# Token tiles moved by indirect transfers of GpSimd in a recurrence and mixture-of-experts kernel

## Chip, core and metric

The kernel runs on one core of a Trainium2 chip. The time is that of the device for one execution, in microseconds (us), and the profile is one execution recorded by the hardware profiler. The engines are TensorE (PE; its weight loads are listed apart as PEld), VectorE (DVE), ScalarE (ACT), GpSimd (POOL) and SyncE (SP). They run side by side, each works through its own instructions in order, and they wait for each other through semaphores. SP does no arithmetic here: it is a queue that issues transfers (DMAs) between the device's memory (DRAM) and the on-chip memory (SBUF). Matmul results go to PSUM, a second on-chip memory in banks.

## The reference

Cut to what is computed, for x of 8 batches, 1024 time steps and 256 features:

```python
xn = layernorm(x)
# online learning: W is changed by each time step
v = einsum('bsd,ed->bse', xn, Wkv[256:]) + bkv[256:]
def step(W, (xt, vt)):                 # xt, vt: 8 x 256, one time step of all batches
    y = xt @ W.T
    gW = (2 / (8 * 256)) * ((y - vt).T @ xt)
    return W - eta * gW, y
s = scan(step, W0, (xn, v))
# 16 linear experts, the best six of each token weighted by a router
probs = softmax(xn @ router_w.T + router_b)
gate = top-6 of probs, normalised, zero elsewhere
g = silu(sum over e of (xn @ expert_w[e]) * gate[:, e])
out = x + s * g
```

## The kernel before

The 8192 tokens go in 64 tiles of 128 rows: a tile is 16 time steps of all 8 batches, with the time step as the slower index, so row r of tile i is batch r mod 8 and time step 16 i + r div 8. In DRAM, x and the output are ordered by batch, then time step; each of the 128 rows of a tile is a run of 1 KB there.

`load(i)` fetches a tile of x by one DMA of the SP queue (line 100). Two tiles share one buffer of the pool `xin`, which has 10 buffers; at the start the same pool holds the raw weights of the 16 experts (`raw`, line 119), so a tile of x takes over the buffer of an expert whose weights have been split. "Splitting" is line 142 (ACT: the high part `hi` is a rounded copy) and line 143 (DVE or POOL: `lo` is the rest); of the expert weights POOL does the odd experts and DVE the even ones. `layernorm(i)` makes statistics on DVE (`st`, `mv`, lines 194 and 196), `ve` and `rstd` on POOL (lines 198, 200) and `xn` on DVE (line 202). From tile 4 on xn is transposed by way of DRAM: blocks by DVE (`xr`, line 208), one DMA out (`bounce`, line 213) and four DMAs back (`xT`, line 215), all on the SP queue.

TensorE then computes, for each tile, the products with the router and value weights (`vr`, `gram`), small matrix solutions for groups of tiles (`q_ps`, `uq_ps`, `z_ps`, `y_ps`), the recurrence (`pe`, `wt_ps`) and the experts in eight pairs (`h`: six matmuls of 512 columns a pair, in one of three PSUM banks). The results of an expert are weighted and summed: most by DVE (`mix`, line 558), six of the 16 by ACT, which writes `part` (line 547, three buffers), and POOL, which adds the parts up (`mix`, line 550). `finish(i)`, placed one pair into the next tile, joins the sums on DVE (`m`, line 568), multiplies on POOL (`my`, line 572), DVE makes `o` (line 574), POOL adds x to it (line 575; DVE for the last tile), and one DMA of the SP queue stores o (line 576).

The order of TensorE and of the SP queue is written out by hand, as places (tile, pair of experts); a scheduler orders DVE, ACT and POOL around it. On SP the events of one place follow each other, so a load can stand behind a store that waits for its tile, and a bounce behind both:

```python
        fetch = max(4, spot - 21)
        if i >= BY_PE:
            put(fetch // 8, fetch % 8, load, i)
    ctx.enter_context(tc.manual_schedule(engines={mybir.EngineType.PE, mybir.EngineType.SP}))
```

Of the kernel before, what the change touches and what calls it, by code (L numbers as in the profile page):

```python
"""Layer norm, then an online-learned linear layer (one gradient step of W per time step) gated by
the silu of a top-6-of-16 mixture of linear experts, with a residual.

Tokens go in tiles of 128 rows: 16 time steps of all 8 batches, time-major. Within a tile the
recurrence is solved exactly: with A = c * X X^T restricted to strictly earlier time steps and
c = eta * 2 / (B * D), the errors of all steps are E = T (X W^T - V), T = (I + A)^-1, where W is the
weight before the tile, and W^T is then lowered by c * X^T E. The state W^T accumulates in one PSUM
bank.

U = T^T is built for a few tiles at a time from diagonal blocks of 32 rows, by Horner's rule  # L10
(I - C (I - C (I - C)), C = A^T), which merge into blocks of 64 and then 128 rows:
U_ab = -U_a C_ab U_b.

TensorE and the DMA queue keep the order given below; the other engines are scheduled around them.
All but the first tiles are transposed without TensorE: in blocks of 32 by VectorE, and the blocks
change places on their way through DRAM.

The large products split each float32 operand exactly into two float32r parts, x = hi + lo, and add
up hi*hi + hi*lo + lo*hi in float32; what is left out is below float32's own rounding.
"""  # L20

# [8 lines left out]
F32 = mybir.dt.float32  # L30
F32R = mybir.dt.float32r
AF = mybir.ActivationFunctionType
ALU = mybir.AluOpType
AX = mybir.AxisListType
PSUM = bass.MemoryType.PSUM

P = 128
# [3 lines left out]
EPS = 1e-10  # L41
# [9 lines left out]
def ttt_moe_kernel(  # L51
# [12 lines left out]
    nc = tc.nc  # L64
    B, S, D = x.shape
    NE = router_w.shape[0]
    KD = D // P
    TS = P // B
    NT = S // TS
# [21 lines left out]
    where = []  # L91
# [3 lines left out]
    x_tiles = {}  # L95

    def load(i):
        if i % 2 == 0:
            x_tiles[i // 2] = xin.tile([P, KD, D], F32, tag="in", name=f"x_{i // 2}")
        nc.sync.dma_start(  # L100
            out=x_tiles[i // 2][:, i % 2, :],
            in_=x[:, i * TS : (i + 1) * TS, :].rearrange("b t d -> t b d"),
        )
# [9 lines left out]

# [1 line left out]
    raws = {}  # L115
# [23 lines left out]
    nc.gpsimd.memset(neg_half, -0.5)  # L139
    # transposed weights: W0^T the first state, [Wv^T | router^T] one moving operand  # L140
    def split(hi, lo, src, engine=None):
# [41 lines left out]

# [1 line left out]
    class Prepared:  # L185
        pass

    tiles = {}

    def layernorm(i):  # L190
        q = tiles[i] = Prepared()
        xt = x_tile(i)
        st = small.tile([P, nc.vector.BN_STATS_DIM], F32, tag="st", name=f"st_{i}")
        nc.vector.bn_stats(st, xt)  # L194
        mv = small.tile([P, nc.vector.BN_AGGR_DIM], F32, tag="mv", name=f"mv_{i}")
        nc.vector.bn_aggr(mv, st)  # L196
        ve = small.tile([P, 1], F32, tag="ve", name=f"ve_{i}")
        nc.gpsimd.tensor_scalar_add(ve, mv[:, 1:2], LN_EPS)  # L198
        rstd = small.tile([P, 1], F32, tag="rstd", name=f"rstd_{i}")
        nc.gpsimd.tensor_tensor(rstd, ve, neg_half, ALU.pow)  # L200
        q.xn = work.tile([P, D], F32, tag="xn", name=f"xn_{i}", bufs=3)
        nc.vector.tensor_scalar(q.xn, xt, mv[:, 0:1], rstd, ALU.subtract, ALU.mult)  # L202
        if i < BY_PE:
            return
        q.xT = work.tile([P, KD * P], F32, tag="xT", name=f"xT_{i}", bufs=3)
        # blocks of 32 are transposed in place, and change places by way of DRAM
        xr = work.tile([P, D], F32, tag="xr", name=f"xr_{i}")
        nc.vector.transpose(
            xr.rearrange("p (c k t) -> p k c t", c=NQ, k=KD),
            q.xn.rearrange("p (k c t) -> p k c t", c=NQ, k=KD),  # L210
        )
        bounce = dram.tile([NQ, Q, NQ, KD * Q], F32, tag="bounce", name=f"bounce_{i}")
        nc.sync.dma_start(out=bounce.rearrange("b d c f -> (b d) (c f)"), in_=xr)
        for c in range(NQ):
            nc.sync.dma_start(
                out=q.xT[at(c), :].rearrange("p (b f) -> p b f", b=NQ),
                in_=bounce[:, :, c, :].rearrange("b d f -> d b f"),
            )
# [17 lines left out]
    def accumulate(o, hi, lo, rhs_hi, rhs_lo, first=True, **kw):  # L236
        # the terms with the moving low part come last: it is ready last
        terms = [t for a, b, r in zip(hi, lo, rhs_hi) for t in ((a, r), (b, r))]
# [6 lines left out]
    def project(i, g, j):  # L245
        q = tiles[i]
        # X X^T = H H^T + H L^T + (H L^T)^T
        gram = misc(f"gram_{i}")
# [29 lines left out]

# [1 line left out]
    layernorm(0)  # L280
# [10 lines left out]

    # -c at strictly earlier time steps, in A's place and in A^T's
    ones = const.tile([P, P], F32)
# [12 lines left out]

    # U and the first half of T by blocks: what is never written stays zero
    u_full, t_half = [], []
# [10 lines left out]
    def open_group(n, first, count):  # L319
# [14 lines left out]
        for name, t in vars(stores[m]).items():  # L334
            if name in ("t", "z2"):
                setattr(g, name, t)
            else:
                setattr(g, name, t[:, j : j + count])
        # odd tiles keep the first half of T, and what comes of it, in the upper partitions
        g.halves = []  # L340
# [7 lines left out]
    def gates(g):  # L348
# [7 lines left out]

        # the six largest logits, the first of equal ones, are marked; two absent values fill up to eight
        lg, top, d, ex = g.lg, wide("top", 8), wide("d"), wide("ex")
# [16 lines left out]
        nc.vector.tensor_reduce(s_top, chosen, AX.X, ALU.add)  # L375
        # gates p / (sum p + EPS) with p = ex / s_all, then divided by max(their sum, EPS)
        nc.vector.scalar_tensor_tensor(den, s_all, EPS, s_top, op0=ALU.mult, op1=ALU.add)
# [11 lines left out]
    def step_q(g, name, rhs, out):  # L389
        """I - C rhs for the diagonal blocks."""  # L390
        c = g.count
# [69 lines left out]
    H = P // 2  # L461
# [24 lines left out]

# [1 line left out]
    def errors_1(i):  # L488
# [74 lines left out]
    def finish(i):  # L563
        # x + y silu(m) = x + (y / 2) m (1 + tanh(m / 2))
        q = tiles[i]
# [9 lines left out]
        (nc.vector if i == NT - 1 else nc.gpsimd).tensor_add(o, o, xt)  # L575
        nc.sync.dma_start(
            out=out[:, i * TS : (i + 1) * TS, :].rearrange("b t d -> t b d"), in_=o
        )

# [1 line left out]
    opened = {}  # L581
# [17 lines left out]

    # what comes before each (tile, pair of experts)  # L600
    events = {}
# [3 lines left out]

    # the first tiles have a schedule of their own: (slot, pair) as 8 * slot + pair
    chain = {
# [85 lines left out]
```

## Time and profile before

| what | value |
|---|---|
| time, median of 2 runs | 1006.72 us (1005.61 to 1007.83) |
| the profiled execution, first to last instruction | 1004.7 us |
| transfers of x | 64, 128 KB each, 2.7 us from issue to landing |
| transfers of the output | 64, 128 KB each, 2.3 us |
| transfers of bounce and xT | 60 of 128 KB (2.4 us), 240 of 32 KB (1.8 us) |
| DMA traffic | 38.65 MB, 38 GB/s in the mean; 231 GB/s in the first fortieth of the span |
| first tile's experts begin on TensorE | 13.05 us; second tile's 37.49 us |

The profiled execution is timed by its span, first to last instruction; the 2.0 us between it and the median of the runs hold what lies around the span and the spread of the runs. In a line of a group, "x64 | 27.1, 425 | 49.9 <-DMA x" means 64 instructions, 27.1 us busy, 425 ns the mean of one, and 49.9 us of idle time of the engine just before them, ended mostly by the transfer named. In a timeline a row has the start and the duration in us, the engine, the line, the operation, output<-input, and in brackets the idle time before it and what ended it.

### The profile page before, as it was taken

Reading aid. Unit: us, or ns where it says so; the run is one execution under the profiler, and the core shown is the slowest. Engines: PE = TensorE matmul, PEld = TensorE weight load, DVE = VectorE, ACT = ScalarE, POOL = GpSimd, SP = SyncE. Lnnn points to the kernel's source line nnn. Section 1 sums busy time; section 2 is a strip of 40 time slices with the busy share of each in tenths; the row PEclk is TensorE's granted clock in tenths of the full one; section 3 lists DMA queues with packets and bytes.
Section 4 is the critical chain, followed back from the end, with each engine's and each line's share of the span. In section 5 each row is a group of like instructions: output and inputs, shape, how many; then the busy total and the mean of one; then the engine's idle time right before and its main releaser. Section 6 shows DMA issues by size and latency. Waiting matters only on the chain.

```text
span 1004.7 us, 19617 instructions
## 1 busy us (share of the span) xinstructions
PE 977.6 (97%) x6672; PEld 799.9 (80%) x6672; DVE 770.0 (77%) x2225; ACT 436.5 (43%) x1174; POOL 440.8 (44%) x677
## 2 busy tenths in 40 slices
PE   5899999999999999999999999999999999999997
PEld 4677888878888887888878888887888878888785
DVE  7888797777878777787777878778787777867665
ACT  5454444344443534435344443534435344443432
POOL 6544344444344344444444344344444444344333
PEclk8899999999999999999999999999999999999999
DMA  7021111111111111111111111011111111100000
GB/s 231 17 53 49 39 27 43 37 27 43 39 27 42 28 37 43 38 27 44 38 28 43 38 28 43 24 42 43 36 29 43 38 28 43 35 25 11 12 11 11
DMA packets 67092, 38.65 MB, mean 38 GB/s; under 512 B 38176, under 2 KB 66992, under 8 KB 66992
## 3 DMA queue, kind: packets, MB, share of 16 engines
q1 hardware_dynamic: 66992, 37.41, 13.6%
q8 instruction: 52, 0.85, 0.3%
q14 instruction: 48, 0.39, 0.1%
HBM read 21.13 MB, written 16.25 MB: 37 GB/s over the span
## 4 chain that ended last, share of the span: by engine, by line
PE 77%; DVE 14%; issue 2%; POOL 2%; DMA 2%; ACT 2%; SPq 1%; POOLq 0%; DVEq 0%; ACTq 0%
PE h L241 59%; PE pe L241 6%; PE wt_ps L241 4%; PE vr L241 3%; DVE q L407 3%; DVE mix L558 2%; DMA x<-in_L_attn_x_dram 1%; PE gram L250 1%; DVE marked L366 1%; POOL mix L550 1%; DVE st L194 1%; ACT part L547 1%; DVE o L574 1%; DVE d L362 1%; PE uq_ps L395 1%
## 5 line engine op out<-in xcount | busy, mean ns | idle before, releaser
L241 PE MATMUL h<-we,xT_two 128*128 128x512 f32 x3072 | 789.3, 402 | 4.5 <-DVE mix L558 2.5
L241 PEld LDWEIGHTS h<-we,xT_two 128*128 128x128 f32 x3072 | 554.5, 189 | 120.1 <-issue 2.7
L558 DVE SCALAR_TENSOR_TENSOR mix<-h,gate,mix 128x256 f32<-128x256 f32 x576 | 265.6, 475 | 112.0 <-PE h L241 80.1
L547 ACT ACTIVATE part<-h,gate 128x256 f32<-128x256 f32 x384 | 182.1, 474 | 293.1 <-DVE mix L558 171.4
L550 POOL TENSOR_TENSOR mix<-mix,part 128x256 f32<-128x256 f32 x256 | 188.7, 737 | 131.4 <-ACT part L547 124.0
L572 POOL TENSOR_TENSOR my<-m,hy 128x256 f32<-128x256 f32 x64 | 47.3, 739 | 159.0 <-DVE m L568 159.0
L550 POOL TENSOR_TENSOR mix<-part,part 128x256 f32<-128x256 f32 x64 | 47.9, 749 | 72.3 <-ACT part L547 72.3
L575 POOL TENSOR_TENSOR o<-o,x 128x256 f32<-128x256 f32 x63 | 46.5, 738 | 69.4 <-DVE lg L263 59.2
L194 DVE BATCH_NORM_STATS2 st<-x 128x6 f32<-128x256 f32 x64 | 27.1, 425 | 49.9 <-DMA x<-in_L_attn_x_dram 49.5
L241 PE MATMUL vr<-w_vr,xT_two 128*128 128x272 f32 x384 | 59.2, 290 | 0.0
L202 DVE TENSOR_SCALAR xn<-x,mv,rstd 128x256 f32<-128x256 f32 x64 | 49.0, 765 | 12.2 <-POOL rstd L200 11.9
L143 DVE TENSOR_TENSOR wt_lo<-wt_ps,wt_hi 128x512 fp32r<-128x512 f32 x64 | 42.9, 671 | 19.6 <-ACT wt_hi L142 19.5
L142 ACT CAST xT_two<-xT 128x256 fp32r<-128x256 f32 x60 | 24.4, 407 | 71.9 <-PE h L241 69.9
L198 POOL TENSOR_SCALAR ve<-mv 128x1 f32<-128x1 f32 x64 | 14.5, 228 | 91.2 <-DVE mv L196 56.4
L143 POOL TENSOR_TENSOR xn_lo<-xn,xn_hi 128x256 fp32r<-128x256 f32 x64 | 47.7, 746 | 14.2 <-ACT xn_hi L142 13.9
L142 ACT CAST p_hi<-p 128x256 fp32r<-128x256 f32 x64 | 26.0, 406 | 63.6 <-DVE p L498 63.5
L241 PEld LDWEIGHTS vr<-w_vr,xT_two 128*128 128x128 f32 x384 | 52.4, 191 | 0.0
L510 ACT ACTIVATE step_hi<-pe,neg_c 128x256 fp32r<-128x256 f32 x64 | 30.4, 474 | 50.5 <-PE pe L241 50.2
L241 PEld LDWEIGHTS pe<-wt_hi,xT_two 128*128 128x128 f32 x256 | 39.2, 189 | 5.9
L142 ACT CAST wt_hi<-wt_ps 128x512 fp32r<-128x512 f32 x64 | 37.2, 581 | 10.8 <-PE wt_ps L241 10.3
L241 PE MATMUL pe<-wt_hi,xT_two 128*128 128x256 f32 x256 | 40.7, 281 | 0.0
L143 DVE TENSOR_TENSOR p_lo<-p,p_hi 128x256 fp32r<-128x256 f32 x64 | 39.2, 612 | 0.9 <-ACT p_hi L142 0.4
(115 smaller groups left out, 1186.7 us busy)
## 6 DMA issues: line engine op xcount, KB each, us to landing
x<-in_L_attn_x_dram SPq DMA_DIRECT2D x64, 128.0 KB, 2.7
out_dram<-o SPq DMA_DIRECT2D x64, 128.0 KB, 2.3
bounce<-xr SPq DMA_DIRECT2D x60, 128.0 KB, 2.4
xT<-bounce SPq DMA_DIRECT2D x240, 32.0 KB, 1.8
raw<-in_L_ffn_expert_w_dram SPq DMA_DIRECT2D x16, 256.0 KB, 5.0
w_raw<-in_L_attn_Wkv_dram SPq DMA_DIRECT2D x1, 256.0 KB, 3.1
w_raw<-in_L_attn_W_dram SPq DMA_DIRECT2D x1, 256.0 KB, 5.2
bias<-in_L_attn_bkv_dram SPq DMA_DIRECT2D x1, 128.0 KB, 4.5
```

Source lines behind the costliest of these rows:

```text
L142: nc.scalar.copy(hi, src)
L143: (engine or nc.vector).tensor_sub(lo, src, hi.bitcast(F32))
L194: nc.vector.bn_stats(st, xt)
L202: nc.vector.tensor_scalar(q.xn, xt, mv[:, 0:1], rstd, ALU.subtract, ALU.mult)
L241: nc.tensor.matmul(o, lhsT=a, rhs=b, start=first and m == 0, stop=(m == len(terms) - 1), **kw)
L407: nc.vector.tensor_add(g.q1[at(b)], g.a[at(b), :, 1, at(b)], ident_q[at(b), :].unsqueeze(1).broadcast_to([Q, c, Q]),)
L510: nc.scalar.mul(q.step_hi, e, neg_c)
L547: nc.scalar.mul(part, he, gate)
L550: nc.gpsimd.tensor_add(new, q.mix[1], part)
L558: nc.vector.scalar_tensor_tensor(new, he, gate, q.mix[j], op0=ALU.mult, op1=ALU.add)
L572: nc.gpsimd.tensor_mul(my, m, q.hy)
L575: (nc.vector if i == NT - 1 else nc.gpsimd).tensor_add(o, o, xt)
```

## The change

All 64 loads of x and all 64 stores of the output leave the SP queue and become indirect transfers that POOL issues: the 128 rows of a tile are addressed by a column of row numbers in SBUF, in x and in the output seen as 8192 rows of 1 KB. The table of row numbers (`rows`, 128 x 64, one column a tile) is made at the start by two `iota` of POOL and five integer operations of DVE: (r mod 8) * 1024 + 16 i + r div 8. The places of loads and stores in the written order stay in the code, but since only TensorE and SP keep that order, the scheduler now places them among POOL's other work. Comments are dropped as well, which moves line numbers (lines of the changed kernel are 14 to 16 higher).

```diff
+I32 = mybir.dt.int32
...
     def load(i):
         if i % 2 == 0:
             x_tiles[i // 2] = xin.tile([P, KD, D], F32, tag="in", name=f"x_{i // 2}")
-        nc.sync.dma_start(
-            out=x_tiles[i // 2][:, i % 2, :],
-            in_=x[:, i * TS : (i + 1) * TS, :].rearrange("b t d -> t b d"),
+        nc.gpsimd.indirect_dma_start(
+            out=x_tiles[i // 2][:, i % 2, :], out_offset=None,
+            in_=x.rearrange("b s d -> (b s) d"),
+            in_offset=bass.IndirectOffsetOnAxis(ap=rows[:, i : i + 1], axis=0),
         )
...
+    part = const.tile([P, NT], I32)
+    nc.gpsimd.iota(part, pattern=[[0, NT]], base=0, channel_multiplier=1)
+    rows = const.tile([P, NT], I32)
+    nc.vector.tensor_single_scalar(rows, part, B - 1, op=ALU.bitwise_and)
+    nc.vector.tensor_single_scalar(rows, rows, 10, op=ALU.logical_shift_left)
+    nc.vector.tensor_single_scalar(part, part, 3, op=ALU.logical_shift_right)
+    steps = const.tile([P, NT], I32)
+    nc.gpsimd.iota(steps, pattern=[[TS, NT]], base=0, channel_multiplier=0)
+    nc.vector.tensor_tensor(part, part, steps, op=ALU.bitwise_or)
+    nc.vector.tensor_tensor(rows, rows, part, op=ALU.bitwise_or)
...
         (nc.vector if i == NT - 1 else nc.gpsimd).tensor_add(o, o, xt)
-        nc.sync.dma_start(
-            out=out[:, i * TS : (i + 1) * TS, :].rearrange("b t d -> t b d"), in_=o
-        )
+        nc.gpsimd.indirect_dma_start(
+            out=out.rearrange("b s d -> (b s) d"),
+            out_offset=bass.IndirectOffsetOnAxis(ap=rows[:, i : i + 1], axis=0),
+            in_=o, in_offset=None,
+        )
```

## The prediction

> **What bounds the kernel now.** I read the busy times first, then a table of windows, then the waits, then the order in time of the places the change touches. Busy times of the whole profiled execution:
>
> ```profile
> span 1004.7 us, 19617 instructions
> PE 977.6 (97%) x6672; PEld 799.9 (80%) x6672; DVE 770.0 (77%) x2225; ACT 436.5 (43%) x1174; POOL 440.8 (44%) x677
> ```
>
> PE is idle for 27.1 us in all (1004.7 - 977.6): that is the most that any relief of waits could give. The windows show where (busy us of each engine, granted clock, DMA share, GB/s):
>
> ```profile
> 0.00:15.00 15.00, 6.40 (x22) 4.84 (x23) 8.56 (x18) 8.20 (x19) 9.25 (x24) 1.00 0.78 239
> 15.00:30.00 15.00, 11.50 (x67) 8.39 (x66) 14.18 (x41) 8.88 (x25) 9.08 (x10) 0.77 0.56 156
> 30.00:45.00 15.00, 11.73 (x60) 8.79 (x59) 14.16 (x48) 5.91 (x19) 9.57 (x19) 0.91 0.07 20
> ...
> 150.00:210.00 60.00, 59.78 (x415) 49.08 (x415) 46.37 (x136) 25.76 (x69) 26.54 (x41) 1.00 0.14 36
> ```
>
> From 150 us on PE lacks 0.22 us in 60: nothing is left to win there, and POOL has 33.5 of 60 us free. The first 45 us are another kernel: PE lacks 15.4 us of it, DVE is full (14.18 and 14.16 of 15), and POOL is busy for 9 to 10 of 15 with the splits of the expert weights. Two waits concern the moved transfers; first all engines, then the SP queue's own (us in total, times, longest):
>
> ```profile
> DVE st L194 <- DMA x<-in_L_attn_x_dram: 49.5, 41, 3.5
> ```
>
> ```profile
> SPq L576 <- POOL o L575: 616.8, 63, 15.6
> ```
>
> SP stands at the store of a tile for most of the kernel, and the next x load is queued behind it, so DVE waits for x. The change ends both. But PE's 0.22 us in 60 says how little of the 49.5 us reaches PE: over some 900 us at most 3 us. I take 1 us off.
>
> **What is added, and its price.** The built order of the changed kernel has 128 transfers on POOL (64 gathers, 64 scatters). Ahead of the first gather come two index patterns on POOL and five integer operations on DVE, each of 64 columns; DVE is idle until 3.49 us, so they cost only a later first gather, inside the terms below. SP loses 128 issues of about 0.6 us, with its 616.8 us of waiting; nothing on SP was late for PE, so that removal is worth nothing beyond the 1 us.
>
> No POOL transfer is in this trace, so its time on POOL is bounded by rows. From below: SP's own issue of the same 128 KB, 0.60 us (median of the x loads). From above: POOL's longest instruction, a 512-column split at 1.63 us; and far above, 2.7 us, from issue to landing, if POOL were held until the data is there. I take 1.5 us: POOL needs 0.739 us for a 256-column two-input operation that DVE does in 0.417 (m, L568), a factor of 1.77, which makes 1.06 us of SP's 0.60; to it comes a pass over one column of indices, on POOL between 0.228 us (ve) and 0.573 us (rstd), 0.4 in the middle.
>
> The Trainium skill (DMA: Bandwidth & Descriptors, "Latency and other measured facts") gives about 1 us to the first byte of a transfer whose descriptors GpSimd writes, against about 0.6 us for one issued by SP; as an estimate of POOL's time, 1.0 us in place of 1.5 would make the sum below 1021 us in place of 1031.
>
> **The start.** This is where the price falls. POOL before:
>
> ```profile
> 7.71 0.73 POOL L143 TENSOR_TENSOR xn_lo<-xn,xn_hi 128x256 fp32r<-128x256 f32 x1 [2.60 <-ACT xn_hi L142]
> ...
> 22.39 0.22 POOL L198 TENSOR_SCALAR ve<-mv 128x1 f32<-128x1 f32 x1 [3.07 <-DVE total L379]
> ...
> 28.21 1.29 POOL L143 TENSOR_TENSOR we<-raw,we 128x512 fp32r<-128x512 f32 x1 [0.63 <-ACT we L142]
> 29.46 0.73 POOL L550 TENSOR_TENSOR mix<-part,part 128x256 f32<-128x256 f32 x1
> 30.79 0.74 POOL L550 TENSOR_TENSOR mix<-mix,part 128x256 f32<-128x256 f32 x1 [0.59 <-ACT part L547]
> ```
>
> In the built order the loads run far ahead: 12 gathers stand before the last expert split on POOL, 16 before the first sum of two parts (29.46 above), 20 before the second (30.79). Twenty at 1.5 us are 30 us. What can hide them is POOL's waiting in this stretch: 0.70 + 2.60 + 0.38 + 1.19 + 0.67 + 3.07 + 1.46 + 0.63 + 0.59 = 11.3 us if all of it can be used; but these are waits for ACT, DVE and landings that stay in part, and only the first two (3.3 us) lie ahead of the first split. So the second sum is late by 18.7 to 26.7 us, 22.7 in the middle. Also, some gathers reuse the buffer of an expert's raw weights and wait, in POOL's queue, for DVE's split of it; the next splits stand behind them. Before PE feels it there is slack: the second sum ends at 31.53 and frees the buffer for the fifth part, which ACT begins at about 32.2 (0.7 us), and that pair's PSUM bank is wanted next by pair 7, whose matmuls begin at 35.90, 3.1 us after the fifth part ends. 22.7 - 0.7 - 3.1 = 19 us late on PE. Nothing takes it back: from 60 us on PE is full.
>
> The gathers may also hold up DVE. In this stretch two tiny additions show what POOL's splits do to it:
>
> ```profile
> 16.83 2.49 POOL L143 TENSOR_TENSOR we<-raw,we 128x512 fp32r<-128x512 f32 x2
> ...
> 17.20 2.17 DVE L407 TENSOR_TENSOR q<-a,ident_q 32x32 f32<-32x32 f32 x2
> ```
>
> The 32x64 form of these takes 0.215 us elsewhere, so two lost about 1.74 us in 2.49 us of POOL. If a gather did the same, 1.5 us of it would cost up to 1.05 us, 21 us for twenty; nothing at all if it doesn't. I take a quarter, 5 us, since few DVE instructions have two such inputs.
>
> The Trainium skill (SBUF — State Buffer, "Who interferes with whom") says that a DVE instruction with two SBUF inputs is blocked by a GpSimd instruction that reads SBUF, not by one that only writes; the row agrees for the splits, and by the page a transfer that writes descriptors would cost DVE nothing, 1026 us in place of the sum below. The page has a rule against the change as well: GpSimd can't write descriptors while DVE runs a 2-port operation; no row here shows its price.
>
> **The steady state.** On POOL the scatter follows the last addition to o, and in every second tile two gathers follow it, ahead of the first sum of the next tile. Before:
>
> ```profile
> 513.28 0.74 POOL L575 TENSOR_TENSOR o<-o,x 128x256 f32<-128x256 f32 x1 [1.34 <-DVE lg L263]
> 515.28 0.79 POOL L550 TENSOR_TENSOR mix<-part,part 128x256 f32<-128x256 f32 x1 [1.26 <-ACT part L547]
> ```
>
> Three transfers from 514.05 put that sum at 518.55 and its end at 519.3. Its first part's buffer is the one of three that ACT's fourth part takes at 519.59: met by 0.3 us. So at 1.5 us the steady state pays nothing, and the point from which it pays is (519.59 - 0.74 - 514.05) / 3 = 1.6 us.
>
> **The end.** The last scatter is issued by POOL, 1.5 us in place of SP's 0.54, and nothing hides it: +1 us.
>
> **Sum.** 19 + 5 + 0 + 1 - 1 = 24 us on the profiled 1004.7 us. That execution lies 2.0 us below the median of 1006.72, so I add 2.0: 1031 us.
>
> **Rivals.** (1) Cheap transfers, not slower by what can be told: at 0.6 us twenty gathers are 12 us against 11.3 us of waiting. What stays is the order on DVE: tile 0's normalisation now stands behind the split of expert 6, whose weights were issued at 8.41 and take 5.2 us; about 1.2 us earlier without the x loads before them, then 0.62 (ACT) + 0.68 (DVE) and 1.9 of norm, transpose and split put the first gram at 15.8, not 10.99. That is 5 us: 1012 us. Up to 1.3 us a transfer, where the terms above are 15 + 5 + 1 - 1 = 20 us, the result stays within 2% (1027 us). For it: POOL's 56% idle. Against: its idle time is not in the first 30 us. (2) Dear transfers: above 1.6 us each clump of three also delays the steady state. At 2.1 us the sum ends 1.5 us late in each of the 22 clumps left after the start: 33 us, with a start of 42 - 3.3 - 3.8 = 35 us (only the first two waits as cover), 5 of DVE and 1 of the end: 1081 us. At 2.7 us it is 3.3 x 22 = 73, and 47 + 5 + 1: 1133 us. (3) The freed SP queue wins: tiles are never late, PE loses its 3 us of waits, and DVE's freed time shortens the start as well; 1003 us if only the 3 us go, and 2% takes 20 of the 27.1 us. Against: the start gets more work. That the change does nothing is excluded by the built order.
>
> **Chances.** Forecast (1.3 to 1.6 us a transfer, and DVE's term between nothing and its 21 us: 1027 to 1050 us) 0.44; cheap 0.32; dear 0.18; SP's gain 0.06, half of it beyond 2%. So faster 0.03, same 0.35, slower 0.62; 2% is about what a measurement of this kernel can tell from no change. The range 1012 to 1085 us reaches from the cheap end to transfers of 2.1 us; it leaves out the third rival and the dearer half of the second, 0.15.
>
> **What would show it.** The POOL transfers' own duration: 1.3 to 1.6 us, or not. The first sum of tile 0, before at 29.46, at 45 to 52. Tile 1's first expert matmul, before at 37.49, some 20 to 25 us later, and the same distance at 210 us and at 900 us: a constant offset is the start, a growing one the steady state. DVE's wait for x gone, and PE no fuller by it. DVE's tiny additions near gathers at 0.2 us or at 1: the lock. I am wrong if POOL turns out to spend under 1 us on a transfer, or if PE's lateness at 60 us is under 10 us.

## The result and the profile after

The changed kernel takes 1021.09 us (median of 2 runs, 1019.91 to 1022.26) where the kernel before took 1006.72: a ratio of 1.014, with a 95% interval of 1.009 to 1.018. That is a loss of 14 us, below the 2% that counted as slower and inside the predicted range of 1012 to 1085 us; the predicted 1031 us was 10 us too high. The profiled execution spans 1020.5 us, 15.8 more than the one before.

The busy times of the whole execution:

```profile
span 1020.5 us, 19596 instructions
...
PE 978.6 (96%) x6672; PEld 798.6 (78%) x6672; DVE 770.8 (76%) x2230; ACT 435.2 (43%) x1174; POOL 574.8 (56%) x807
```

PE does the same work in almost the same time (977.6 us before); 14.8 of the 15.8 us are time in which PE stands. POOL has 134 us more, and these two groups make it up (busy us, mean ns of one; then POOL's idle time just before them and what ended it):

```profile
L590 POOL DMA_INDIRECT out_dram<-o,rows x64 | 70.6, 1102 | 21.5 <-POOL o L589 17.5
...
L101 POOL DMA_INDIRECT x<-in_L_attn_x_dram,rows x64 | 64.8, 1013 | 18.4 <-issue 14.4
```

A scatter holds POOL for 1.10 us, a gather for 1.01. The idle time before them belongs to the price: 48 of the 64 gathers have 0.30 us in front of them in which nothing is waited for ("issue"). In a row they therefore follow each other every 1.25 to 1.40 us.

The windows show where PE waits (busy us of each engine, granted clock, DMA share, GB/s):

```profile
0.00:15.00 15.00, 1.71 (x6) 0.93 (x6) 7.84 (x17) 8.26 (x17) 10.95 (x27) 1.00 0.82 248
15.00:30.00 15.00, 8.59 (x46) 6.72 (x47) 14.75 (x33) 6.53 (x15) 12.46 (x14) 1.00 0.48 148
30.00:45.00 15.00, 11.39 (x65) 8.24 (x66) 11.17 (x38) 5.70 (x22) 12.90 (x16) 0.89 0.25 71
150.00:210.00 60.00, 59.76 (x417) 48.96 (x416) 47.66 (x139) 26.09 (x70) 36.30 (x51) 1.00 0.13 38
```

In the first 15 us PE has 1.71 us of work where it had 6.40; POOL has gone from 9 to almost 13 of 15 us in the next two, and much of the rest are the gaps before gathers. From 150 us on PE is as full as before (59.78), although POOL does 10 us more in each 60. This is the timeline of POOL at the start (start, duration, line, operation, in brackets the idle time before):

```profile
33.56 0.95 POOL L101 DMA_INDIRECT x<-in_L_attn_x_dram,rows  x1 [0.30 <-issue]
34.54 2.51 POOL L157 TENSOR_TENSOR we<-raw,we 128x512 fp32r<-128x512 f32 x2
...
43.06 0.82 POOL L564 TENSOR_TENSOR mix<-part,part 128x256 f32<-128x256 f32 x1
44.05 1.02 POOL L101 DMA_INDIRECT x<-in_L_attn_x_dram,rows  x1 [0.17 <-POOL mix L564]
45.37 0.96 POOL L101 DMA_INDIRECT x<-in_L_attn_x_dram,rows  x1 [0.30 <-issue]
...
47.89 1.09 POOL L101 DMA_INDIRECT x<-in_L_attn_x_dram,rows  x1 [0.30 <-issue]
49.00 1.60 POOL L214 TENSOR_TENSOR rstd<-ve,neg_half 128x1 f32<-128x1 f32 x3
50.58 0.71 POOL L564 TENSOR_TENSOR mix<-mix,part 128x256 f32<-128x256 f32 x1
```

The last two splits of the weights (`we`) begin with 34.54 (26.32 and 28.21 before), the first sum of tile 0 at 43.06 (29.46), the second, after four more gathers, at 50.58 (30.79). In the middle of the run a scatter and two gathers stand in a row ahead of a sum:

```profile
514.21 1.10 POOL L590 DMA_INDIRECT out_dram<-o,rows  x1 [0.29 <-POOL o L589]
515.61 1.10 POOL L101 DMA_INDIRECT x<-in_L_attn_x_dram,rows  x1 [0.30 <-issue]
517.01 0.96 POOL L101 DMA_INDIRECT x<-in_L_attn_x_dram,rows  x1 [0.30 <-issue]
...
518.04 0.74 POOL L564 TENSOR_TENSOR mix<-part,part 128x256 f32<-128x256 f32 x1
```

The distance between the kernels, tile by tile, says what each stage is worth. Below, "late" is always the start of a tile's first expert matmul (`h`) minus the same in the kernel before: 9.8 us at tile 0, 16.2 at tile 1, 13.6 at tile 3, 17.0 at tile 5, 16.7 at tiles 7 to 12, and then slowly less, 14.7 at the last. The last 1.1 us of the span come after the last matmul.

### The profile page after: what moved, and what is told of

Its sections match the earlier page's. It is cut to its first block, busy times and chain, and to the rows that moved or that the text cites. A ratio compares the mean times of both kernels' runs of the same rounds, so it can differ in the third digit from the quotient of the medians.

```text
span 1020.5 us, 19596 instructions
## 1 busy us (share of the span) xinstructions
PE 978.6 (96%) x6672; PEld 798.6 (78%) x6672; DVE 770.8 (76%) x2230; ACT 435.2 (43%) x1174; POOL 574.8 (56%) x807
## 4 chain that ended last, share of the span: by engine, by line
PE 88%; DVE 6%; issue 2%; POOL 2%; ACT 1%; DMA 1%; SPq 1%; POOLq 0%; DVEq 0%; ACTq 0%
PE h L255 68%; PE pe L255 6%; PE wt_ps L255 4%; PE vr L255 4%; PE gram L264 2%; DVE q L421 1%; POOL x L101 1%; PE gram L282 1%; DVE mix L572 1%; DMA raw<-in_L_ffn_expert_w_dram 1%; PE z_ps L480 1%; PE y_ps L465 1%; PE y_ps L491 1%; PE q_ps L409 1%; PE uq_ps L409 1%
## 5 line engine op out<-in xcount | busy, mean ns | idle before, releaser
L572 DVE SCALAR_TENSOR_TENSOR mix<-h,gate,mix 128x256 f32<-128x256 f32 x576 | 268.7, 477 | 121.6 <-PE h L255 111.5
L590 POOL DMA_INDIRECT out_dram<-o,rows x64 | 70.6, 1102 | 21.5 <-POOL o L589 17.5
L101 POOL DMA_INDIRECT x<-in_L_attn_x_dram,rows x64 | 64.8, 1013 | 18.4 <-issue 14.4
L564 POOL TENSOR_TENSOR mix<-part,part 128x256 f32<-128x256 f32 x64 | 47.7, 746 | 15.8 <-ACT part L561 14.3
L526 DVE SCALAR_TENSOR_TENSOR step_lo<-pe,neg_c,step_hi 128x256 fp32r<-128x256 f32 x64 | 30.9, 483 | 17.7 <-ACT step_hi L524 17.2
L157 DVE TENSOR_TENSOR p_lo<-p,p_hi 128x256 fp32r<-128x256 f32 x64 | 41.6, 650 | 1.9 <-ACT p_hi L156 1.0
```

Source lines behind the costliest of these rows:

```text
L101: nc.gpsimd.indirect_dma_start(out=x_tiles[i // 2][:, i % 2, :], out_offset=None, in_=x.rearrange("b s d -> (b s) d"), in_offset=bass.Indi ...
L157: (engine or nc.vector).tensor_sub(lo, src, hi.bitcast(F32))
L526: nc.vector.scalar_tensor_tensor(q.step_lo, e, neg_c, q.step_hi.bitcast(F32), op0=ALU.mult, op1=ALU.subtract)
L564: nc.gpsimd.tensor_add(new, q.mix[1], part)
L572: nc.vector.scalar_tensor_tensor(new, he, gate, q.mix[j], op0=ALU.mult, op1=ALU.add)
L590: nc.gpsimd.indirect_dma_start(out=out.rearrange("b s d -> (b s) d"), out_offset=bass.IndirectOffsetOnAxis(ap=rows[:, i : i + 1], axis=0), ...
```

## The experiments

Each was timed or profiled beside the kernel before on the same chip. The diffs are against the changed kernel. One table holds all that the text draws on: lateness in us at seven tiles, the number of POOL transfers, how much longer the span is than the 1004.7 us of before, and the time with its ratio to before (95% interval).

| kernel | tile 0 | 1 | 3 | 7 | 12 | 44 | 63 | transfers | span | time, ratio |
|---|---|---|---|---|---|---|---|---|---|---|
| after | 9.8 | 16.2 | 13.6 | 16.7 | 16.7 | 14.1 | 14.7 | 128 | +15.8 | 1021.1, 1.009–1.018 |
| stores_pool | 0.8 | 2.1 | 1.1 | 1.2 | 1.1 | 1.9 | 1.2 | 64 | +5.2 | 1011.6, 1.003–1.006 |
| loads_pool | 9.3 | 15.6 | 12.4 | 13.4 | 14.0 | 18.2 | 17.4 | 64 | +19.1 | 1025.2, 1.015–1.020 |
| late20 | 1.5 | 1.6 | 1.6 | 1.8 | 6.6 | 6.1 | 6.1 | 108 | +13.6 | 1019.5, 1.009–1.014 |
| first4_sp | 1.4 | 13.6 | 10.9 | 12.5 | 12.5 | 10.2 | 10.8 | 124 | +11.7 | 1018.6, 1.009–1.014 |
| paced | 9.7 | 11.8 | 11.4 | 22.2 | 21.9 | 19.9 | 20.6 | 128 | +21.6 | 1026.8, 1.016–1.020 |
| paced_first4 | 0.2 | -0.3 | 2.1 | 12.6 | 12.6 | 10.6 | 11.3 | 124 | +12.3 | 1020.2, 1.010–1.014 |
| paced32 | 9.4 | 10.6 | 10.2 | 13.2 | 14.3 | 11.8 | 12.4 | 128 | +13.9 | 1020.9, 1.013–1.017 |
| paced32_first8 | 1.2 | 1.3 | 1.2 | 4.1 | 4.7 | 4.0 | 4.4 | 120 | +5.2 | 1011.6, 1.003–1.007 |
| extra2 | 8.1 | 15.3 | 12.8 | 15.7 | 15.3 | 11.9 | 11.4 | 172 | +15.5 | 1021.5, 1.011–1.015 |
| plain_pool | 2.6 | 8.0 | 4.8 | 3.9 | 4.7 | 10.9 | 11.1 | 128 | +11.9 | 1014.5, 1.004–1.007 |
| plain_loads | 2.9 | 8.4 | 6.3 | 5.8 | 6.3 | 10.1 | 10.6 | 128 | +11.6 | 1018.7, 1.010–1.013 |
| last12_sp | 9.0 | 15.4 | 12.8 | 15.9 | 15.6 | 13.1 | 13.6 | 116 | +13.5 | 1019.9, one run |

### One half of the change at a time

stores_pool gives the loads back to SP (first part of the diff), loads_pool the stores (second part):

```diff
     def load(i):
-        nc.gpsimd.indirect_dma_start(
...
+        nc.sync.dma_start(
+            out=x_tiles[i // 2][:, i % 2, :],
+            in_=x[:, i * TS : (i + 1) * TS, :].rearrange("b t d -> t b d"),
         )
...
     def finish(i):
-        nc.gpsimd.indirect_dma_start(
...
+        nc.sync.dma_start(
+            out=out[:, i * TS : (i + 1) * TS, :].rearrange("b t d -> t b d"), in_=o
         )
```

> Only the output stores are indirect transfers of POOL; x is loaded by SP as before. Theory (the loss is the start: gathers of x queued on POOL ahead of the expert splits and the first sums): no gather, so no late start, TensorE within 2 us of the kernel before at 210 us, the freed SP queue gives back 1 to 3 us by the end, the last scatter costs 1 us: 1004 to 1008 us. Rival (64 scatters of about 1.1 us delay POOL's sums in every tile): an offset that grows from tile to tile, 1010 us or more.

> Only the loads of x are indirect transfers of POOL; the output is stored by SP as before. Theory: the whole late start stays, TensorE 15 to 18 us late at 210 us, and the end has SP's store again: 1018 to 1023 us. Rival (the scatters carry half of the loss or more): 1014 us or less.

The loads carry the lateness: 15.6 us at tile 1 with the loads alone, 2.1 with the stores alone. Both kernels are slower than I expected. For stores_pool the reason lies behind the last matmul: PE ends 1.2 us late, but the span is 5.2 us longer. The other 4.0 us are a drain of POOL, to which I come at the end. In loads_pool the lateness grows from 13.4 to 18.2 us. At tiles 10, 14, 18 and so on, every fourth, it gains 0.3 to 0.7 us, where PE waits for `step_lo` of DVE; what makes DVE late there I did not follow.

### Taking the gathers away from the start

late20 leaves x of the first 20 tiles to plain transfers of SP; first4_sp does so for the first four, with 4 in place of 20:

```diff
     def load(i):
+        if i < 20:
+            nc.sync.dma_start(
+                out=x_tiles[i // 2][:, i % 2, :],
+                in_=x[:, i * TS : (i + 1) * TS, :].rearrange("b t d -> t b d"),
+            )
+        else:
             nc.gpsimd.indirect_dma_start(
```

> The first 20 tiles of x are loaded by SP, the other 44 by gathers of POOL, all stores by scatters of POOL. Theory (only the gathers of the start cost): as with stores alone, 1003 to 1008 us, with three transfers on POOL after every second tile hidden. Rival (the clumps of three transfers cost in the steady state): an offset that grows by 0.2 us or more in every second tile from tile 20 on, 1012 us or more.

> The first 4 tiles of x are loaded by SP, the rest and the stores as in the changed kernel: tile 0 is normalised before the expert splits again, but 16 gathers still stand on POOL ahead of the second sum, 10 ahead of the last split. Theory A (the pile on POOL sets the loss): 16 at 1.28 us are 20 us against 7 us of cover and 4 us of slack, TensorE 7 to 12 us late at 210 us, 1012 to 1017 us. Theory B (the late first tile and DVE's order set it): at most 3 us late at 210 us, 1004 to 1009 us.

first4_sp tells the two causes at the start apart. Tile 0 is nearly on time again (1.4 us late), so what made it late went with the gathers of the first four tiles: their own time, the table that they wait for, or the order of the work around them. But tile 1 is 13.6 us late all the same, with 16 gathers ahead of tile 0's second sum. The pile of gathers costs by itself.

late20 has no gathers at the start and is 1.5 to 2.1 us late up to tile 8, as stores_pool is without any gather. Then it jumps by almost 5 us. POOL's timeline there:

```profile
167.87 1.35 POOL L107 DMA_INDIRECT x<-in_L_attn_x_dram,rows  x1 [0.17 <-issue]
...
174.54 0.95 POOL L107 DMA_INDIRECT x<-in_L_attn_x_dram,rows  x1 [0.30 <-issue]
175.51 0.75 POOL L595 TENSOR_TENSOR o<-o,x 128x256 f32<-128x256 f32 x1
176.21 0.74 POOL L570 TENSOR_TENSOR mix<-part,part 128x256 f32<-128x256 f32 x1
```

Six gathers stand in a row here, and the finished tile and the first sum behind them. The pile had only moved, which I had not expected; the steady state behind it costs nothing (6.6 us late at tile 12, 6.1 at tile 63).

### Letting the gathers go two at a time

If rows of gathers are the cause, spreading them must help. In paced the gathers of tiles 8 to 19 get their row numbers from a copy that DVE makes from the joined sums `m` of an earlier tile (masked to zero, so that the numbers stay the same); no scheduler can put them ahead of it. paced_first4 also leaves x of tiles 0 to 3 to SP.

```diff
     def load(i):
+        index, c = (held, i % 2) if 8 <= i < 20 else (rows, i)
+        if 8 <= i < 20 and i % 2 == 0:
+            late = small.tile([P, 2], I32, tag="late", name=f"late_{i}", bufs=2)
+            nc.vector.tensor_single_scalar(
+                late, joined[(i - 8) // 2][:, :2].bitcast(I32), 0, op=ALU.bitwise_and
+            )
+            held = small.tile([P, 2], I32, tag="held", name=f"held_{i}", bufs=2)
+            nc.vector.tensor_tensor(held, late, rows[:, i : i + 2], op=ALU.bitwise_or)
+            index = held
...
-            in_offset=bass.IndirectOffsetOnAxis(ap=rows[:, i : i + 1], axis=0),
+            in_offset=bass.IndirectOffsetOnAxis(ap=index[:, c : c + 1], axis=0),
```

> As changed, but the gathers of x for tiles 8 to 19 take their row numbers from a copy of the table's columns that DVE makes only after it has joined the sums of tile 0, 1, 2 ... 5 (one pair of gathers a tile), so that the scheduler can't put them ahead of tile 0's sums. Theory (the pile): 12 of the 20 gathers leave the stretch before tile 0's sums; the first tile stays 9 to 10 us late, and the lateness of the experts at tiles 5 to 12 falls from 16.7 us to 9 to 11; time 1012 to 1016. Rival one (order of the first tile's work alone makes the lateness): tiles 5 to 12 stay 15 to 17 us late, time 1019 to 1022. Rival two (a gather costs TensorE wherever it stands): the lateness grows by more than 0.5 us a tile from tile 1 to tile 6.

> As paced, and x of tiles 0 to 3 by plain transfers of the SP queue, so that only four gathers stand ahead of tile 0's sums. Theory (pile and first tile's order together make all of the lateness): 1 to 2 us late at tile 0, 2 to 4 at tiles 5 to 12, 2 us less at the end; time 1006 to 1010. Rival (the pile moves to where the gathers are let go, as it did with tiles 0 to 19 by SP): 6 us or more late from tile 2 on, time 1012 to 1015.

Up to tile 3 both do what the theory of the pile says: 11.4 us instead of 13.6 in paced, and 2.1 or less in paced_first4, where neither cause is left at tile 1. At tile 6 both jump by 7 us, and both end slower than expected. POOL's timeline of paced_first4 shows a new row:

```profile
141.41 1.10 POOL L119 DMA_INDIRECT x<-in_L_attn_x_dram,held  x1 [0.18 <-issue]
...
144.07 0.95 POOL L119 DMA_INDIRECT x<-in_L_attn_x_dram,rows  x1 [0.30 <-issue]
...
151.68 0.95 POOL L119 DMA_INDIRECT x<-in_L_attn_x_dram,rows  x1 [0.30 <-issue]
152.66 0.73 POOL L582 TENSOR_TENSOR mix<-part,part 128x256 f32<-128x256 f32 x1
```

Behind the last held pair come the gathers of tiles 20 to 25, whose buffers had been free for a while: eight gathers and a scatter, 11 us, ahead of a sum. PE stands for 5.3 us meanwhile and goes on 1.3 us after that sum's start (148.66 to 153.95). So the hold had to go on. paced32 carries it on to tile 31; in paced32_first8 x of tiles 0 to 7 goes by SP, and a pair is let go by the finished output tile `o` instead of `m`.

```diff
-        index, c = (held, i % 2) if 8 <= i < 20 else (rows, i)
-        if 8 <= i < 20 and i % 2 == 0:
+        index, c = (held, i % 2) if 8 <= i < 32 else (rows, i)
+        if 8 <= i < 32 and i % 2 == 0:
```

> As paced, with the hold carried on to tile 31 (one pair of gathers a tile from tile 1 to 12). In paced eight gathers (tiles 18 to 25) stood in a row behind the last hold at 142 to 152 us of its sister run and put TensorE 7 us back at tile 6. Theory (what costs is gathers in a row ahead of a sum, wherever they stand): the jump at tile 6 is gone, lateness at tiles 7 to 12 is 14 to 16 us instead of 22, end 12 to 15, time 1017 to 1021. Rival (each held pair costs where it stands): lateness goes on growing by 0.5 us or more a tile to tile 12, past 18.

> As paced32, but x of tiles 0 to 7 by plain transfers of the SP queue, and the held gathers are let go by the finished output tile, so that they stand behind its store; no gather stands ahead of tile 0's sums. 120 transfers of GpSimd in all. Theory (the lateness is all from transfers ahead of sums in the first tiles): 0 to 3 us late at tiles 1 to 12, 2 us less at the end, GpSimd's last drain 3 to 4 us; time 1005 to 1009, the time before within 0.3%. Rival (a store and two gathers in a row in every tile, not every second one, is more than the sums can bear): growth of 0.5 us or more a tile up to tile 12, time 1011 to 1015.

The jump at tile 6 is gone: 13.2 us late at tile 7 in paced32 against 22.2 in paced. In paced32_first8 the lateness is 1.3 us at tile 1. Both are as slow as they are for reasons that stand apart: paced32 has the late first tile still, and both gain 2 to 3 us at one place, pair 3 of tile 4. The change has 2.1 us there too, first4_sp 2.1, loads_pool 1.5; stores_pool and late20, without gathers at that time, have 0.5, and the two kernels with plain loads on POOL (below) nothing. In the trace of the change PE waits there for 2.0 us for `t` of ACT, beside a scatter and two gathers on POOL (118.04 to 121.71). ACT's `u` just ahead of `t`, DVE's `xx`, and the sum:

```profile
120.84 0.52 ACT L471 COPY u<-y_ps 32x128 f32<-32x128 f32 x2 [3.81 <-PE h L255]
...
120.88 0.29 DVE L290 TENSOR_TENSOR xx<-gram,cross 128x128 f32<-128x128 f32 x1 [2.10 <-PE h L255]
...
122.16 0.72 POOL L564 TENSOR_TENSOR mix<-part,part 128x256 f32<-128x256 f32 x1 [0.45 <-issue]
```

It isn't the sum that holds things up: it begins 0.45 us after the last gather, when ACT's part is there. `u` and `xx` begin 2.2 and 2.0 us after the trace has the matmuls that they read as ended (118.63 and 118.88); before it was 0.06 and 0.04 us, in plain_pool and plain_loads 0.1 or less. Why indirect transfers go with this delay at this place alone is open. paced32_first8 is the best version with gathers, at 1011.6 us; it does not beat the kernel before.

### Twice the clump

The prediction had said that the steady state pays from 1.6 us a transfer on, that is, when the three of a clump take 4.8 us. extra2 adds two gathers into spare buffers (the second of half rows) behind each pair of loads from tile 20 on, let go by the same output tile:

```diff
+        if i >= 20 and i % 2 == 1:
...
+            nc.vector.tensor_tensor(held, late, rows[:, i : i + 1], op=ALU.bitwise_or)
+            for n in range(2):
+                spare = extra.tile([P, D >> n], F32, tag=f"spare{n}", name=f"spare{n}_{i}")
+                nc.gpsimd.indirect_dma_start(
+                    out=spare, out_offset=None,
+                    in_=x.rearrange("b s (n d) -> (b s n) d", d=D >> n),
+                    in_offset=bass.IndirectOffsetOnAxis(ap=held, axis=0),
+                )
```

> As changed, and two more gathers into spare buffers behind each pair of loads from tile 20 on (22 pairs), let go by the same output tile that lets the pair go: 172 transfers in all, clumps of a store and four gathers with one sum among them. Theory (what a clump may take before TensorE waits was 4.8 us to the first sum, about 6.7 us to the second): 5 transfers by 1.27 to 1.4 us and a sum of 0.8 us are 7.1 to 7.8 us, so 0.4 to 1.1 us of TensorE per pair of tiles, 9 to 24 us at the end, time 1030 to 1046. Rival (the cover is deeper than read): lateness does not grow, time 1020 to 1025.

The scheduler put the first sum between the pair of loads and the extra gathers, so that it still waits for three transfers only; the limit that is passed is that of the second sum. POOL's timeline (the scatter and the first gather, not shown, lie before it, and the addition to o ends at 511.63):

```profile
514.80 1.02 POOL L104 DMA_INDIRECT x<-in_L_attn_x_dram,rows  x1 [0.30 <-ACT part L578]
...
515.88 0.75 POOL L581 TENSOR_TENSOR mix<-part,part 128x256 f32<-128x256 f32 x1
516.80 0.97 POOL L118 DMA_INDIRECT spare<-in_L_attn_x_dram,held  x1 [0.16 <-DVE den L408]
518.07 0.95 POOL L118 DMA_INDIRECT spare<-in_L_attn_x_dram,held  x1 [0.30 <-issue]
519.03 0.75 POOL L581 TENSOR_TENSOR mix<-mix,part 128x256 f32<-128x256 f32 x1
...
520.43 1.56 POOL L581 TENSOR_TENSOR mix<-mix,part 128x256 f32<-128x256 f32 x2
```

The second sum begins 7.4 us after the addition, where the theory had given it about 6.7. After the extra gathers POOL works without a break and has caught up 3 us later. PE is busy for 60.00 of 60 us from 210 to 270, and the lateness does not grow: it falls, from 15.3 us at tile 12 to 11.4 at the last. So the theory's second limit falls; its first, 4.8 us to the first sum, is not put to the test (4.0 to 4.3 us from the end of the addition in the steady state, here and in the change). A scatter and four gathers with a sum among them fit in the steady state; rows of gathers at the start do not.

### The price: queue or row numbers

plain_pool issues the same 128 transfers on POOL without row numbers. plain_loads, the last run, does so for the loads alone.

```diff
     def load(i):
-        nc.gpsimd.indirect_dma_start(
...
+        nc.gpsimd.dma_start(
+            out=x_tiles[i // 2][:, i % 2, :],
+            in_=x[:, i * TS : (i + 1) * TS, :].rearrange("b t d -> t b d"),
         )
```

> As changed, but the 128 transfers are plain ones (the access patterns of the SP queue's, no row numbers) issued by GpSimd. Theory (the price is that of a transfer whose descriptors GpSimd itself writes): 1.0 to 1.1 us each as the indirect ones, lateness at tiles 5 to 12 of 14 to 18 us, time 1018 to 1024. Rival (the price is that of reading row numbers): 0.6 us or less each, lateness 8 or less, time 1009 to 1014.

The groups of plain_pool's two kinds of transfer:

```profile
L101 POOL DMA_DIRECT2D x<-in_L_attn_x_dram x64 | 34.9, 556 | 2.8 <-DVE top L376 2.5 <-issue 0.3
...
L589 POOL DMA_DIRECT2D out_dram<-o x64 | 38.7, 605 | 22.0 <-POOL o L588 17.8
```

A plain load holds POOL for 0.56 us, an indirect one for 1.01; a plain store 0.61, an indirect one 1.10. Before the plain loads there are no gaps ("issue 0.3" in all). So about half of the price goes with the row numbers, and the rival was nearer than the theory: the lateness at tiles 7 to 12 is 3.9 to 4.7 us. Then it grows to 11 us, which neither expected. (The profile is of an execution of 1018.5 us; the other three took 1014.1 to 1014.7, and whether the growth is as large in them isn't known.) At every fourth tile PE waits up to 1.0 us for DVE's `step_lo`. DVE's timeline of plain_pool there:

```profile
324.21 1.60 DVE L290 TENSOR_TENSOR a<-xx,masks 128x256 f32<-128x256 f32 x1
...
327.05 1.03 DVE L420 TENSOR_TENSOR q<-a,ident_q 32x128 f32<-32x128 f32 x2
328.11 0.48 DVE L525 SCALAR_TENSOR_TENSOR step_lo<-pe,neg_c,step_hi 128x256 fp32r<-128x256 f32 x1
```

`a` is 0.42 us long in most tiles. In nine of the 64 it takes 1.60, and in all nine POOL's second load, a small fill and its first sum lie beside it; in the 25 beside a transfer alone it takes 0.424. (By these rows `a` would have ended at 324.63, and the sum begins at 324.74; what begins the hold is not to be seen.) plain_loads was to tell whether it is the sum's place or the plain load:

> As changed, but the loads of x are plain transfers issued by GpSimd; the stores stay indirect. The start is that of plain_pool (same order, loads of 0.56 us), the steady clump takes 0.5 us longer than there. In plain_pool DVE's operation a took 1.60 us in nine tiles where the second load, a small fill and the first sum of GpSimd lay beside it, and 0.42 us beside a transfer alone; TensorE lost 0.8 us each time. Theory (it is the sum's place beside a): the sum moves 0.5 us later, past a, and TensorE's lateness no longer grows between tiles 12 and 44: 4 to 6 us late there and at the end, time 1010 to 1012. Rival (plain loads on GpSimd hold DVE whatever stands behind them): lateness grows by 6 to 7 us again, to 10 to 12 at the end, time 1014 to 1017.

Half of the theory holds. With the sum later by the longer store, `a` is short everywhere (0.43 us in the mean of 40 that lie beside a transfer alone). But the lateness still grows, by 0.5 us at every fourth tile (6.3 us at tile 12, 10.1 at tile 44), and the theory's time, 1010 to 1012 us, is missed by 7. The sum now lies beside the operation that comes next:

```profile
326.88 0.99 DVE L420 TENSOR_TENSOR q<-a,ident_q 32x128 f32<-32x128 f32 x2
327.90 0.59 DVE L390 SCALAR_TENSOR_TENSOR den<-s_all,s_top 128x4 f32<-128x4 f32 x1
```

POOL sums from 326.62 to 327.42 and from 327.67 to 328.47; the first `q` pair takes 0.99 us and `den` 0.59, while the trace of the change has 0.57 and 0.16 for them, with POOL in gathers. That a sum beside them costs is read from the times; no run took the sums away. It suggests that the longer clump of the change is not only a cost: it keeps POOL's sums off this work of DVE in every fourth tile.

### The end

last12_sp gives the last 12 stores to SP:

```diff
-        nc.gpsimd.indirect_dma_start(
+        if i < NT - 12:
+            nc.gpsimd.indirect_dma_start(
...
+        else:
+            nc.sync.dma_start(
+                out=out[:, i * TS : (i + 1) * TS, :].rearrange("b t d -> t b d"), in_=o
+            )
```

> As changed, with the last 12 stores by plain transfers of the SP queue: 116 transfers of GpSimd. Its last drain took 0.8 us with none, 6.1 to 6.5 with 64, 10.1 with 108, 3.5 with 124, 3.6 with 128, 6.7 with 172. Theory (0.09 us for each transfer since the last time that the queue's list was cleared, which falls between the 108th and the 124th): either 2.5 to 3.5 us (cleared before the 116th) or 10.5 to 11.5 us (not yet), nothing between. Rival (it depends on the last transfers alone, which are by SP here): 1 us or less. Lateness of TensorE as changed, 14 to 17 us; time 1017 to 1025.

The records of the trace have a drain of POOL behind its last work, which no view counts as busy. Its time, by the number of POOL transfers in the program, from all the traces:

```
transfers   0      64 loads  64 stores  108    116   120   124   128          172
drain us    0.83   6.08      6.54       10.14  1.67  3.29  3.46  3.64, 3.65   6.71
```

(plain_pool's 128 plain ones: 3.18; plain_loads: 3.64.) From 0 to 108 it is 0.08 to 0.09 us for each transfer; then it falls, and grows again from 116 on. last12_sp gave 1.67 us, which was in none of the ranges that I had set out, so the rule behind it stays open; it isn't about the last transfers alone, since loads_pool made its last one at 732 us and has 6.08. Each number is from one profiled execution.

## Why the prediction came out as it did

The time, 1021 us, lies inside the stated range, but not where the prediction put the most: it is below the forecast's own band (1027 to 1050 us, 0.44) and in that of its cheap rival (1012 to 1027, 0.32), and the loss stays below the 2% that was called slower, which had 0.62.

**The price of a transfer** was taken as 1.5 us, between 0.6 and 2.7. It is 1.0 to 1.1 us busy and 1.25 to 1.40 us in a row: the right neighbourhood, 0.2 us too high. Part of that is luck. The transfer itself was put at 1.06 us, because POOL is 1.77 times as slow as DVE at an addition; a plain transfer holds POOL for 0.56 to 0.61 us, no longer than SP was held (0.60). The surcharge for the row numbers (0.4 us) was near the measured 0.5, and the gap of 0.30 us, which no row of before showed, is part of the price and made up for the rest. The lower estimate of 1.0 us a transfer and 1021 us in all fits both numbers, but it was a time to the first byte, and no run shows that POOL's own time is the same thing.

**The start** was the right place and the right cause, too many gathers on POOL ahead of work that others wait for. It was mis-sized by the price, and the way from POOL to PE was not the one described. Predicted: the second sum of tile 0 late by 18.7 to 26.7 us, PE by 3.8 less, 19 us. Measured: the second sum at 50.58 for 30.79, 19.8 us late; tile 1 late by 16.2 at its first matmul and by 13.6 from tile 2 on. At 1.27 us in a row the twenty gathers are 25.4 us instead of 30, and POOL's waiting covered 25.4 - 19.8 = 5.6 of them, where I had taken 7.3 in the middle.

The 3.8 us of slack rested on a misread row: the second sum was said to free the buffer of the fifth part. It is the first sum that frees those of the fourth and the fifth; the second frees the sixth's. ACT's timeline of the change, with DVE's between:

```profile
44.16 0.82 ACT L561 ACTIVATE part<-h,gate 128x256 f32<-128x256 f32 x2
...
49.62 0.41 DVE L216 TENSOR_SCALAR xn<-x,mv,rstd 128x256 f32<-128x256 f32 x1 [1.47 <-POOL rstd L214]
49.95 1.79 DVE L421 TENSOR_TENSOR q<-a,ident_q 32x32 f32<-32x32 f32 x4
51.77 0.41 DVE L216 TENSOR_SCALAR xn<-x,mv,rstd 128x256 f32<-128x256 f32 x1
...
53.15 0.46 ACT L561 ACTIVATE part<-h,gate 128x256 f32<-128x256 f32 x1
```

The fourth and fifth part run at 44.16, right behind the first sum and 6 us ahead of the second. PE's long wait ahead of tile 1, from 47.87 to 52.34, is for the `xn` that DVE begins at 51.77 (the normalisation of tile 3, which the written order transposes there). On POOL its `rstd` stands in the row of three at 49.00, behind the same last four gathers as the second sum. ACT's sixth part comes after three copies of `xn`, 1.9 us after the second sum has ended, and PE waits another 0.75 us for it. PE's waits for `xn` in the whole run, at tile 0 and here:

```profile
PE xtr L241 <- DVE xn L216: 17.8, 2, 13.3
```

So the pile reaches PE through the normalisation and not through the sums alone, and that 19.8 - 16.2 = 3.6 us is near the predicted 3.8 is luck. In first4_sp both ways show: PE waits 7.1 us for a part behind the first sum, then 4.4 us for `xn`. That the pile is the cause is shown four times: by first4_sp, by the jumps that follow it in late20 and in paced, and by what is left without it in paced32.

**What the sum left out** is the first tile. It was only in the cheap rival, as 5 us of order on DVE. It is 9.8 us at tile 0. The chain that ended last goes through the order that this rival named: a split of expert weights, which landed at 13.8 us, stands on DVE ahead of tile 0's `xn`, and it runs beside POOL's reading operations. DVE's timeline of the change:

```profile
14.48 4.18 DVE L157 TENSOR_TENSOR we<-raw,we 128x512 fp32r<-128x512 f32 x1 [0.96 <-ACT we L156]
18.59 0.40 DVE L216 TENSOR_SCALAR xn<-x,mv,rstd 128x256 f32<-128x256 f32 x1
```

The next split takes 0.68 us (18.91); this one lost 3.5, beside POOL's `rstd`, `we`, `rstd`, `we` from 14.55 to 18.10, which read their operands. Without the split `xn` could have begun at 15.15, against 5.14 before: the first gather waits for the table of row numbers and starts at 4.14 us where SP issued at 0.8, and tile 0's `rstd` stands on POOL behind two gathers. I had called the table free and looked for the lock only beside gathers. The two causes do not add up: without most of the pile (eight gathers ahead of the second sum instead of twenty) tile 1 is 10.6 us late (paced32), without the late first tile 13.6 (first4_sp), with both 16.2, with neither 1.3 (paced32_first8). A late first tile gives POOL time for gathers that it would otherwise owe.

**The lock by gathers**, 5 us in the sum, is nothing. The test that the prediction named, the tiny additions beside gathers, in DVE's timeline (POOL is in gathers from 25.45 to 26.78 and from 27.08 to 28.03):

```profile
25.86 0.39 DVE L421 TENSOR_TENSOR q<-a,ident_q 32x32 f32<-32x32 f32 x2
...
26.59 0.40 DVE L421 TENSOR_TENSOR q<-a,ident_q 32x32 f32<-32x32 f32 x2
```

0.2 us each (the last of the four lies in the gap), where they took over 1 us beside POOL's splits before. In the whole run 41 operations `a` lie beside POOL's transfers alone, 0.423 us in the mean; in the kernel before the 32 with nothing of POOL beside them took 0.424. The rule weighed in the prediction (the Trainium skill, SBUF — State Buffer, "Who interferes with whom": blocked by a GpSimd instruction that reads SBUF, not by one that only writes) would have put the sum at 1026 us; the traces agree with it in both directions, 0.2 us beside gathers and 4.18 beside the reading `we` and `rstd`. An indirect transfer takes a column of row numbers from SBUF too; no hold by that shows.

**The steady state**, 0 in the sum, is right from tile 5 on. A scatter and two gathers put the first sum 4.0 to 4.1 us after the addition to o, less than the 4.8 us of the prediction, so its threshold of 1.6 us a transfer was not reached by any run in the steady state. One clump does cost, the one at tile 4: 3.5 us, 2.1 of them the wait described above. The rest comes with a lower granted clock (0.52 in the profile's window from 124 to 127 us); first4_sp keeps 1.00 there and loses 2.1 us only.

**The x wait** is gone as predicted, 49.5 us to one wait of

```profile
DVE st L208 <- DMA x<-in_L_attn_x_dram,rows: 1.7, 1, 1.7
```

PE gets 2.3 us back between tile 5 and the end (17.0 to 14.7 us late), where I took 1 of at most 3, but for another reason. It comes in steps of 0.2 to 0.7 us at every fourth tile, 10, 14, 18 and so on, where the kernel before waits for DVE's `step_lo` and the change seldom does. Between 250 and 800 us, before and after:

```profile
PE wt_ps L241 <- DVE step_lo L512: 1.7, 6, 0.4
...
PE wt_ps L255 <- DVE step_lo L526: 0.7, 1, 0.7
```

**The end**, +1 us, measured 1.1, also by luck. The last scatter's data land 2.8 us after the last addition for 2.3 with SP's store, half of what I had taken; what ends last is POOL's drain (at 1019.73 us, 0.3 us after SP has seen all landings), which was not in the sum. In stores_pool the same term is 4.0 us.

Together: 19 + 5 + 0 + 1 - 1 = 24 us stand against 13.5 (up to tile 4) + 3.5 (there) - 2.3 + 1.1 = 15.8. Of the rivals, the cheap one came nearest (20 us for 1.3 us a transfer, and the late first tile), the dear one and SP's gain did not come.

## What to carry to other kernels

An operation that moves to an engine with time to spare costs by where the scheduler puts it: look at the built order for the number of moved instructions ahead of the first one that somebody waits for, and price that row, not the total. Loads with nothing to wait for were put first here, all of them; to spread them they had to be tied to the progress of the work, and the tie had to last until the buffers did the same. And follow the row to the engine that matters by every instruction behind it: here the tiny `rstd` carried the delay as much as the sums did. A steady state that has been balanced can have a reserve while its start has none.

## What the runs showed of the hardware

- An indirect transfer of 128 rows of 1 KB holds POOL for 1.01 us (gather) or 1.10 us (scatter), with 0.30 us before most of them in which nothing is waited for; a plain one of the same bytes 0.56 and 0.61 us.
- A program with POOL transfers ended here with a longer drain of POOL: 6.1 to 6.5 us for 64 transfers, 10.1 for 108, but 1.7 to 3.6 for 116 to 128. In stores_pool that is most of the loss. What sets it is open.
- One split of DVE, which has two operands in SBUF, ended 0.6 us after the last of four reading instructions of POOL beside it: 4.18 us for 0.68. Beside POOL's transfers alone DVE's two-operand `a` kept its time: 0.423 us in 41 cases with indirect ones, 0.424 in 25 with plain ones.
- At one place (tile 4) ACT and DVE began 2.0 to 2.2 us after the recorded end of the matmuls that they read, in the change; in the kernel before and with plain loads on POOL it was 0.1 us or less. The cause is open.
